# Two-layer graph kernel on one core: scatters put off around a change of batch group, first gathers spread out

## The chip, the core and the metric

The kernel runs on one core of one Trainium2 chip. The core has five engines that matter here: TensorE (matmuls, PE), VectorE (DVE), ScalarE (ACT), GpSimd (POOL) and SyncE (SP), each with its own instruction queue that is worked off in order, and 16 DMA engines that all of them share. The metric is device time in microseconds for the whole program, the median of several runs. A profiled execution gives the trace from which the profile's views come.

## The reference, cut to what matters

Two graph layers act on `x` of 16 batches x 1024 nodes x 256 features, with one adjacency matrix `adj` of 1024 x 1024 that is mostly zero.

```python
# layer 0: attention with adj as an added bias
feats = einsum('bni,oi->bno', x, W1); f1 = feats @ W2 + b2
coefs = softmax(leaky_relu(f1[:, :, None] + f1[:, None, :]) + adj)
h = coefs @ feats + bias2 + x
# layer 1: edge scores
pre_u = h @ W1[:d]; pre_v = h @ W1[d:]
S = sigmoid(relu(pre_u[:, :, None] + pre_v[:, None] + b1) @ W2 + b2)
a_t = einsum('buv,bud->bvd', S * adj, h)
m_t = einsum('uv,bud->bvd', adj, h) * h
out = beta1*h + beta2*(a_t @ Wa + ba) + beta3*(m_t @ Wm + bm)
```

The score `S` is needed only where `adj` is not zero, so the kernel works it out edge by edge.

## The kernel before, in words

**Stages.** At the start the kernel lists the edges: a table of 21 tiles, each with 128 rows (one row: a node u and up to eight nodes v). The widths of the tiles fall from 8 to 1; together they have 135 *slots*. A slot is 128 edges, one on each partition. Slot 134 is the single column of the last tile.

The 16 batches go through layer 0 one after the other. For each batch the kernel stores what the edge scores need: `pu_d` and `pw_d` (272 numbers for each node and batch: the two halves of the hidden layer, sorted by the sign of the second weight) and `ha_d` (h times Wa). Batches are scored in three groups of 5, 5 and 6 batches (groups 0, 1, 2). A group can be scored when its batches are through layer 0. So the scoring of group 0 runs beside batches 5 to 9, that of group 1 beside batches 10 to 15, and that of group 2 beside the last stage.

In the last stage TensorE does the sums over edges: it reads the scores back as dense blocks (`sat`, from the array `sa_d`, one array for each group), weighs them with `adj` (`apart`) and multiplies them with `ha_g` (matmuls `pzg` and `pzh`). The groups come there in the order 1, 0, 2. The `adj` messages of eight batches (`pm`, `pz`, stored as `zb_d`) were put off to this stage and lie between those matmuls.

**One slot.** For slot k of group g:

- `fetch(g, k)` (GpSimd): an indirect DMA gathers the rows `pw_d[v]` into a buffer `gv` (line 1219). At the first slot of a tile it also gathers `pu_d[u]` into `gu` (line 1212). There are five `gv` buffers (`GV`). Groups 0 and 1 use the same five, group 2 has five of its own in another pool (`wide`).
- `compare(k, 0)` and `compare(k, 1)` (VectorE, line 1248): maximum and minimum of `gv` and `gu`.
- `sums` (ScalarE, line 1262, one instruction for each batch; in every eighth slot of group 2 VectorE, line 1259): the sum over the 272 numbers goes to a column of `lg`.
- When a *part* of slots is complete (parts end at slots 16, 32, 48, 64, 80, 96, 112, 124, 131 and 135), `gates` (ScalarE, line 1270) and `last` (VectorE, line 1289) finish the scores, and `last` puts one scatter for each slot of the part on the list `late`. There are five `lg` buffers.
- `scatter` (GpSimd, line 1228): an indirect DMA writes 128 scores to `sa_d[g]`. The scatters of a group are declared to be independent of each other; against any other access to `sa_d[g]` the framework keeps the program's order.

**What sets the order.** The kernel's engines and queues follow the order in which instructions are emitted, and that order is written by hand. `Timetable` collects entries (time, function) and emits them sorted by time. The times are a planner's estimate; nothing waits for them on the chip. A slot's time is `start + k * (end - start) / 135`. At that time `first` fetches slot k + 3 (`AHEAD`) and issues one scatter from `late`, or two when more than 12 wait. For slot 0 `first` is due 15 us earlier: it fetches slots 0, 1, 2 and 3 at once. The loads of the last stage have times of their own, counted back from the time at which its matmuls begin (`when[0]`), and are issued by SyncE:

```python
for i, p in enumerate(parts):
    due = when[0] - 36.0 + 4.0 * i if i < SA else begins[parts[i - SA]] - 4.0
    ...
    times.at(due, lambda p=p: load_sa(*p))        # line 1332: sat <- sa_d
    times.at(begins[p] - 8.2, lambda p=p: part_sa(*p))    # ScalarE, line 1345
    times.at(begins[p] - 6.0, lambda p=p: weigh_sa(*p))   # VectorE, line 1350
```

`SA` is 7: the first seven loads have buffers of their own. Other instructions that the prediction names: `keep_product` (VectorE, line 1188, `zb`), whose store ScalarE issues (line 1194); `turn_h` (TensorE, line 1080, `ph`); `message` (TensorE, line 1158, `pm`); `keep_turned` (`xT`); `load_ha` (SyncE, line 1318, `ha_g`) and `take_up` (SyncE, line 1151, `xh`). DMAs of SyncE and ScalarE share eight lanes in turn; an issue waits until its lane's DMA before has landed. GpSimd's DMAs have eight lanes as well.

Of the kernel before, what the change touches and what calls it, by code (L numbers as in the profile page):

```python
# [29 lines left out]
SLOTS = [(t, s) for t, width in enumerate(WIDTHS) for s in range(width)]  # L30
# [341 lines left out]
def edge_layers(  # L372
# [40 lines left out]
    NG = len(GROUPS)  # L413
# [18 lines left out]
    first = first_stack.enter_context(tc.tile_pool(name="first", bufs=1, side="right"))  # L432
# [80 lines left out]
    for i in range(H):  # L513
# [5 lines left out]
        for o in range(H):  # L519
# [4 lines left out]
                start=(o == 0),  # L524
# [20 lines left out]
    many = const.tile([P, 2], F32, name="many")  # L545
# [655 lines left out]

    PARTS = [16, 32, 48, 64, 80, 96, 112, 124, 131, len(SLOTS)]
    AHEAD = GV - 2
    HA = 9
    SA = 7
    late = []

    def fetch(g, k):
        t, s = SLOTS[k]
        if s == 0:  # L1210
            gu = st["gu", t] = pools["gath", g].tile([P, SIZE[g] * R], F32, name="gu", bufs=2)
            nc.gpsimd.indirect_dma_start(
                out=gu,
                out_offset=None,
                in_=pu_d[g],
                in_offset=bass.IndirectOffsetOnAxis(ap=key_u[:, t : t + 1], axis=0),
            )
        gv = st["gv", k] = pools["gath", g].tile([P, SIZE[g] * R], F32, name="gv", bufs=GV)
        nc.gpsimd.indirect_dma_start(  # L1219
            out=gv,  # L1220
            out_offset=None,
            in_=pw_d[g],
            in_offset=bass.IndirectOffsetOnAxis(ap=idx_v[:, t, s : s + 1], axis=0),
        )

    def scatter(g, lg, i, k):
        t, s = SLOTS[k]
        dma = nc.gpsimd.indirect_dma_start(  # L1228
            out=sa_d[g],
            out_offset=bass.IndirectOffsetOnAxis(ap=idx_s[:, t, s : s + 1], axis=0),  # L1230
            in_=lg[:, i, : SIZE[g]],
            in_offset=None,
            bounds_check=N * N - 1,
            oob_is_err=False,
        )
        tc.declare_no_dep(dma.ins, group=f"sa{g}", reason="edges of their own")
        tc.add_to_no_dep_group(f"sa{g}", dma.ins)
# [4 lines left out]
    def compare(k, half):  # L1242
        if k in [0, *PARTS] and half == 0:
            st["lg"] = dense.tile([P, PARTS[0], MOST], F32, name="lg", bufs=5)
        cols, op = ((slice(0, HALF), ALU.max), (slice(HALF, R), ALU.min))[half]
        mv = by_batch(st["gv", k])[:, :, cols]
        mu = by_batch(st["gu", SLOTS[k][0]])[:, :, cols]
        nc.vector.tensor_tensor(mv, mv, mu, op)  # L1248

    def place_of(k):  # L1250

        part = next(i for i, end in enumerate(PARTS) if k < end)
        return (PARTS[part - 1] if part else 0), PARTS[part]

    def sums(k, js, lg):
        one = by_batch(st["gv", k])
        i = k - place_of(k)[0]
        if len(js) == one.shape[1]:
            nc.vector.tensor_reduce(lg[:, i, : len(js)], one, AX.X, ALU.add)
        else:  # L1260
            for j in js:
                nc.scalar.activation(  # L1262
                    one[:, j, :], one[:, j, :], AF.Copy, accum_out=lg[:, i, j : j + 1]
                )

    def gates(g, k, lg):

        k0, k1 = place_of(k)
        part = lg[:, : k1 - k0, : SIZE[g]]
        nc.scalar.activation(part, part, AF.Tanh, bias=b2_h, scale=0.5)  # L1270

    def scores(g, start, end, on_vector):

        for k in range(len(SLOTS)):
            time = start + k * (end - start) / len(SLOTS)

            def first(k=k):
                for n in range(AHEAD) if k == 0 else ():
                    fetch(g, n)
                if k + AHEAD < len(SLOTS):  # L1280
                    fetch(g, k + AHEAD)
                for _ in range(min(len(late), 2 if len(late) > PARTS[0] - 4 else 1)):
                    late.pop(0)()

            def last(k=k):
                k0, k1 = place_of(k)
                lg = st["lg", k0]
                part = lg[:, : k1 - k0, : SIZE[g]]
                nc.vector.tensor_scalar(part, part, 1.0, None, ALU.add)
                late.extend(lambda i=i: scatter(g, lg, i, k0 + i) for i in range(k1 - k0))  # L1290

            times.at(time - (15.0 if k == 0 else 0.0), first)
            times.at(time + 0.1, lambda k=k: compare(k, 0))
            times.at(time + 0.9, lambda k=k: compare(k, 1))
            k0, k1 = place_of(k)
            if k == k0:
                times.at(time + 0.2, lambda k0=k0: st.update({("lg", k0): st["lg"]}))
            summed = lambda js, k=k, k0=k0: sums(k, js, st["lg", k0])
            if on_vector(k):
                times.at(time + 1.7, lambda f=summed: f(range(SIZE[g])))  # L1300
            else:
                for j in range(SIZE[g]):
                    times.at(time + 2.0 + 0.6 * j, lambda f=summed, j=j: f((j,)))
            if k + 1 == k1:
                times.at(time + 5.4, lambda k=k, k0=k0: gates(g, k, st["lg", k0]))
                times.at(time + 6.0, last)
        ended = end + 4.0
        if g + 1 == NG:
            times.at(ended, lambda: [late.pop(0)() for _ in range(len(late))])
        return ended  # L1310
# [5 lines left out]
    def load_ha(g, c):  # L1316
        st["ha", g, c] = pools["late"].tile([P, CUT * D], F32, name="ha_g", bufs=HA)
        nc.sync.dma_start(
            out=st["ha", g, c], in_=ha_d[g][c * P : (c + 1) * P, : CUT * D]
        )  # L1320
# [133 lines left out]
    def products(b, *ids):  # L1454
        for i in ids:
            time = times.matmuls(4 * D, lambda i=i: product(b, i))
            times.at(time + 0.3, lambda i=i: keep_product(b, i))
            times.at(time + 2.3, lambda i=i: store_product(b, i))
        return time + 1.0

    times = Timetable()
# [148 lines left out]
    for n in range(3):  # L1610
# [4 lines left out]
        time = products(b, 2, 3)  # L1615
# [65 lines left out]
    for g in range(NG):  # L1681
        ended = scores(g, paced[g], paced[g + 1], lambda k, g=g: g + 1 == NG and k % 8 == 3)
# [22 lines left out]
    for n, (g, c) in enumerate((g, c) for g in order for c in range(C)):  # L1705
        if n < C:
            due = opened + 2.0 + (when[0] - 14.0 - opened) * n / C
        elif n < HA:
            due = when[2 + n - C] + 0.1
        else:  # L1710
            k, c1 = divmod(n - HA, C)
            due = begins[order[k], C - 1, c1] + 2.4
# [18 lines left out]
@with_exitstack  # L1731
def tile_graph_layers(ctx: ExitStack, tc: tile.TileContext, *args):
    nc = tc.nc
    I32 = mybir.dt.int32
    hold = ctx.enter_context(tc.tile_pool(name="hold", bufs=1))
    flag = hold.tile([1, 1], I32, name="flag")
    edge_layers(tc, *args, flag)
    over = nc.values_load(
        flag[0:1, 0:1],
        min_val=0,  # L1740
        max_val=1,
        skip_runtime_bounds_check_because="it is a comparison's result",
    )
    with tc.If(over > 0):
        dense_layers(tc, *args)
# [43 lines left out]
```

## Time and profile before

| | before |
|---|---|
| median of 3 runs (lowest to highest) | 2082.96 us (2081.66 to 2084.3) |
| profiled execution | 2087.25 us |
| its span, first to last instruction | 2085.5 us |
| PE busy | 2023.7 us, 97% |
| VectorE, ScalarE, GpSimd busy | 1569.9, 1374.0, 1137.4 us |
| granted TensorE clock, mean | 0.997 |
| gathers `gv`, GpSimd | 405, 1204 ns each |
| scatters `sa_d`, GpSimd | 405, 1257 ns each |
| comparisons, VectorE | 810, 909 ns each |
| HBM traffic over the span | 308 GB/s |

An entry such as "DVE gv L1248 <- DMA gv<-pw_d,idx_v: 106.1, 55, 12.0" in the list of waits means: VectorE's instruction of line 1248, which writes `gv`, waited for a DMA into `gv`, 106.1 us in all, in 55 places, at most 12.0 us. In a view in order of time each line has the start, the duration, engine, line, operation, output <- inputs, the number of instructions merged, and in brackets the idle time before it and what ended it. PEclk is the share of the clock that TensorE was granted. The DMA share is how busy the 16 DMA engines were. Idle time of an engine costs nothing by itself; it counts only where TensorE or the end of the program waits for it.

### The profile page before, as it was taken

What the parts mean: (1) busy time and instruction counts of PE and PEld (TensorE: products, weight loads), DVE (VectorE), ACT (ScalarE), POOL (GpSimd) and SP (SyncE); (2) the same over time, 40 slices, a digit from 0 to 9 for tenths busy, and PEclk for the clock granted to TensorE, in tenths of its full rate; (3) what the DMA queues carried; (4) which work ended last, traced back from release to release, by engine and by line L of the source; (5) the groups of instructions that cost most, each with busy time, mean ns of one, the idle gap of its engine ahead of it and who ended that gap; (6) DMA issues with size and microseconds to landing.
All of it is one profiled execution on the core that took longest, in us unless ns stands there. A gap on an engine that the chain in (4) does not pass through costs nothing.

```text
span 2085.5 us, 28967 instructions
## 1 busy us (share of the span) xinstructions
PE 2023.7 (97%) x8577; PEld 1551.1 (74%) x8577; DVE 1569.9 (75%) x2348; ACT 1374.0 (66%) x4842; POOL 1137.4 (55%) x974
## 2 busy tenths in 40 slices
PE   8999999999999999999999999899999989999998
PEld 6888887777776868677888886457676666768887
DVE  7799884677877777677878886578888878885544
ACT  4211222577777767687888777577888878886654
POOL 1122221267676767678777777666767766773000
PEclk9999999999999999999999999999999999999999
DMA  6689776788888889789999989899999999997773
GB/s 219 244 310 347 286 294 244 255 262 285 286 279 270 282 283 293 262 293 297 318 300 323 328 302 312 317 396 414 382 392 366 412 415 397 387 402 265 282 234 123
DMA packets 250007, 644.37 MB, mean 309 GB/s; under 512 B 38642, under 2 KB 139762, under 8 KB 247794
## 3 DMA queue, kind: packets, MB, share of 16 engines
q0 software_dynamic: 82016, 348.87, 47.7%
q1 hardware_dynamic: 132002, 259.36, 33.8%
q10 hardware_dynamic: 35824, 34.22, 4.7%
q8 instruction: 69, 1.13, 0.2%
q14 instruction: 96, 0.79, 0.1%
HBM read 479.56 MB, written 162.92 MB: 308 GB/s over the span
## 4 chain that ended last, share of the span: by engine, by line
PE 53%; DMA 18%; DVE 12%; ACT 8%; issue 6%; POOL 3%; SPq 0%; ACTq 0%; POOLq 0%; DVEq 0%
PE pv L1060 16%; DMA gv<-pw_d,idx_v 10%; PE pm L1158 9%; PE pp L1098 7%; PE pzg L1363 6%; DVE gv L1248 5%; PE pf L1006 4%; ACT gv L1262 4%; PE pea L1126 3%; DMA sat<-sa_d 3%; PE pzh L1363 3%; PE pz L1178 2%; ACT apart L1345 2%; DMA ha_g<-ha_d 2%; POOL sa_d L1228 2%
## 5 line engine op out<-in xcount | busy, mean ns | idle before, releaser
L1262 ACT ACTIVATE gv<-gv 128x272 f32<-128x272 f32 x2058 | 856.1, 419 | 308.2 <-DVE gv L1248 202.3
L1248 DVE TENSOR_TENSOR gv<-gv,gu 128x680 f32<-128x680 f32 (+1 forms) x810 | 706.5, 909 | 110.5 <-DMA gv<-pw_d,idx_v 106.1
L1219 POOL DMA_INDIRECT gv<-pw_d,idx_v x405 | 487.6, 1204 | 307.3 <-ACT gv L1262 197.0
L1228 POOL DMA_INDIRECT sa_d<-lg,idx_s x405 | 509.2, 1257 | 135.1 <-issue 109.5
L1060 PE MATMUL pv<-feats,eT 128*128 128x257 f32 x2048 | 468.9, 381 | 7.3 <-DVE eT L1047 6.7
L1158 PE MATMUL pm<-adj_sb,xh 128*128 128x512 f32 x1024 | 450.9, 593 | 1.7 <-DVE xh L1074 1.7
L1060 PEld LDWEIGHTS pv<-feats,eT 128*128 128x128 f32 x2048 | 381.1, 189 | 71.4 <-DVE eT L1047 14.9
L1262 ACT ACTIVATION_READ_ACCUMULATOR gv<-gv 128x1 f32 x2058 | 388.9, 189 | 0.0
L1363 PE MATMUL pzg<-ha_g,apart 128*128 128x256 f32 x1536 | 367.1, 382 | 22.2 <-DVE apart L1350 21.8
L1158 PEld LDWEIGHTS pm<-adj_sb,xh 128*128 128x128 f32 x1024 | 193.6, 191 | 220.2 <-issue 217.6
L1363 PEld LDWEIGHTS pzg<-ha_g,apart 128*128 128x128 f32 x1536 | 288.3, 190 | 83.6 <-DVE apart L1350 36.9
L1345 ACT COPY apart<-sat 128x640 f32<-128x640 f32 (+1 forms) x192 | 264.6, 1392 | 82.8 <-PE pzh L1363 38.7
L1350 DVE TENSOR_TENSOR apart<-apart,adj_sb 128x640 f32<-128x640 f32 (+1 forms) x192 | 166.3, 868 | 130.0 <-ACT apart L1345 129.4
L1098 PE MATMUL pp<-wuv,hT 128*128 128x272 f32 x1024 | 250.4, 394 | 6.7 <-ACT end L1112 3.8
L1098 PEld LDWEIGHTS pp<-wuv,hT 128*128 128x128 f32 x1024 | 194.6, 191 | 53.4 <-issue 6.2
L1047 DVE SCALAR_TENSOR_TENSOR eT<-row,col,grown 128x512 f32<-128x512 f32 x256 | 183.0, 746 | 24.6 <-ACT col L993 23.8
L852 POOL DMA_INDIRECT table_d<-rec,at x52 | 57.4, 1105 | 252.2 <-DVE rec L845 154.9
L1091 ACT COPY hT<-ph 128x512 f32<-128x512 f32 x96 | 55.2, 576 | 109.3 <-PE ph L1080 109.1
L1126 PE MATMUL pea<-wa,hT 128*128 128x256 f32 x512 | 121.4, 380 | 0.0
L1178 PE MATMUL pz<-wm,mT 128*128 128x256 f32 x512 | 116.0, 379 | 0.2 <-DVE mT L1169 0.2
L1006 PE MATMUL pf<-w1T,xT 128*128 128x257 f32 x512 | 114.1, 380 | 0.9 <-DVE xT L964 0.9
L1363 PE MATMUL pzh<-ha_g,apart 128*128 128x256 f32 x384 | 114.2, 379 | 0.0
(179 smaller groups left out, 1588.6 us busy)
## 6 DMA issues: line engine op xcount, KB each, us to landing
sa_d<-zero SPq DMA_DIRECT2D x128, 512.0 KB, 5.7
sat<-sa_d SPq DMA_DIRECT2D x128, 320.0 KB, 9.3
sat<-sa_d SPq DMA_DIRECT2D x64, 384.0 KB, 4.8
pu_d<-end SPq DMA_DIRECT2D x64, 272.0 KB, 4.9
pw_d<-end SPq DMA_DIRECT2D x64, 272.0 KB, 5.9
ha_d<-ea SPq DMA_DIRECT2D x64, 256.0 KB, 6.0
zb_d<-zb ACTq DMA_DIRECT2D x64, 256.0 KB, 6.8
xh<-in_x_dram SPq DMA_DIRECT2D x15, 1024.0 KB, 12.4
```

The lines of the kernel that those rows point to most:

```text
L1006: nc.tensor.matmul(pfs[i], lhsT=st["xT"][:, h, c * P : (c + 1) * P], rhs=w1T[:, h, :], start=(h == 0), stop=(h == H - 1),)
L1047: nc.vector.scalar_tensor_tensor(st["eT", b, k, n][:, i, :], st["row"][:, cols], st["col"][:, j : j + 1], grown[:, j, cols], ALU.max, ALU. ...
L1060: nc.tensor.matmul(pv[:, : D + 1], lhsT=st["eT", b, k, j // 4][:, j % 4, i * P : (i + 1) * P], rhs=st["feats", b][:, j, :], start=(j == 0) ...
L1098: nc.tensor.matmul(pp[:, k, :R], lhsT=st["hTi", b, i][:, h, k * P : (k + 1) * P], rhs=wuv[:, side, h, :], start=(h == 0), stop=(h == H - 1),)
L1126: nc.tensor.matmul(pp[:, k, :], lhsT=st["hTi", b, i][:, h, k * P : (k + 1) * P], rhs=wa[:, h, :], start=(h == 0), stop=(h == H - 1),)
L1158: nc.tensor.matmul(pm, lhsT=held[b][:, c, h * P : (h + 1) * P], rhs=adj_sb[:, c, span], start=(c == 0), stop=(c == C - 1),)
L1219: nc.gpsimd.indirect_dma_start(out=gv, out_offset=None, in_=pw_d[g], in_offset=bass.IndirectOffsetOnAxis(ap=idx_v[:, t, s : s + 1], axis=0),)
L1228: dma = nc.gpsimd.indirect_dma_start(out=sa_d[g], out_offset=bass.IndirectOffsetOnAxis(ap=idx_s[:, t, s : s + 1], axis=0), in_=lg[:, i, : ...
L1248: nc.vector.tensor_tensor(mv, mv, mu, op)
L1262: nc.scalar.activation(one[:, j, :], one[:, j, :], AF.Copy, accum_out=lg[:, i, j : j + 1])
L1345: nc.scalar.copy(apart.rearrange("p g v -> p v g"), sat)
L1363: nc.tensor.matmul(st["pzg", g, vc][j // 4][:, j % 4, :], lhsT=apart[:, j, :], rhs=ha, start=(c == 0 and j % 2 == 0), stop=(c == C - 1 and ...
```

## The change

Three things change in `scores`.

1. In groups 0 and 1, `first` issues no scatter in the last 14 slots (`HUSH`, slots 121 to 134).
2. In groups 1 and 2, `first` issues two scatters a slot in slots 0 to 15, as long as any are left.
3. Slots 0, 1 and 2 are fetched by entries of their own. In groups 1 and 2 they are due 15.0, 11.5 and 8.0 us before the start and the fetch of slot 3 comes with slot 0 at the start itself; in group 0 they stay together, about 15 us before it.

```diff
+    HUSH = 14
...
             def first(k=k):
-                for n in range(AHEAD) if k == 0 else ():
-                    fetch(g, n)
                 if k + AHEAD < len(SLOTS):
                     fetch(g, k + AHEAD)
-                for _ in range(min(len(late), 2 if len(late) > PARTS[0] - 4 else 1)):
+                if k + HUSH >= len(SLOTS) and g + 1 < NG:
+                    return
+                many = len(late) > PARTS[0] - 4 or (g and k < PARTS[0])
+                for _ in range(min(len(late), 2 if many else 1)):
                     late.pop(0)()
...
-            times.at(time - (15.0 if k == 0 else 0.0), first)
+            if k < AHEAD:
+                ahead = 15.0 - (3.5 * k if g else 0.01 * k)
+                times.at(start - ahead, lambda k=k: fetch(g, k))
+            times.at(time - (0.0 if g or k else 14.9), first)
```

## The prediction

> **What bounds the kernel now.** First I read the busy rows, then the waits, then TensorE, VectorE, GpSimd and SyncE in order of time around the two changes of group, then the table of stretches. TensorE works for 2023.7 us of the 2085.5 us span, so whatever the change gives must come out of TensorE's idle time. The list of waits (total us, times, longest) names the two kinds that matter:
>
> ```profile
> DVE gv L1248 <- DMA gv<-pw_d,idx_v: 106.1, 55, 12.0
> ...
> PE pzg L1363 <- DVE apart L1350: 21.8, 30, 1.8
> ...
> PE ph L1080 <- DVE zb L1188: 7.1, 2, 5.7
> ```
>
> The 7.1 us lie at the change from group 1 to group 2. TensorE there (start, us, work, wait before it):
>
> ```profile
> 1331.03 7.03 PE L1158 MATMUL pm<-adj_sb,xh 128*128 128x512 f32 x16
> 1343.79 1.11 PE L1080 MATMUL ph<-ident,xh 128*128 128x128 f32 x4 [5.73 <-DVE zb L1188]
> 1346.29 1.12 PE L1080 MATMUL ph<-ident,xh 128*128 128x128 f32 x4 [1.38 <-DVE zb L1188]
> 1347.19 8.04 PE L1158 MATMUL pm<-adj_sb,xh 128*128 128x512 f32 x16
> ```
>
> Two waits, and after them a message of 8.04 us instead of 7.03. VectorE was late because of one gather, and GpSimd's order shows which:
>
> ```profile
> 1338.58 3.48 DVE L1248 TENSOR_TENSOR gv<-gv,gu 128x680 f32<-128x680 f32 x4 [12.02 <-DMA gv<-pw_d,idx_v]
> ```
>
> ```profile
> 1318.25 0.95 POOL L1212 DMA_INDIRECT gu<-pu_d,key_u  x1 [0.30 <-issue]
> 1319.51 0.94 POOL L1219 DMA_INDIRECT gv<-pw_d,idx_v  x1 [0.30 <-issue]
> 1320.75 1.54 POOL L1219 DMA_INDIRECT gv<-pw_d,idx_v  x1 [0.30 <-issue]
> 1322.60 0.94 POOL L1219 DMA_INDIRECT gv<-pw_d,idx_v  x1 [0.30 <-issue]
> 1323.84 0.93 POOL L1219 DMA_INDIRECT gv<-pw_d,idx_v  x1 [0.31 <-issue]
> 1325.08 1.59 POOL L1228 DMA_INDIRECT sa_d<-lg,idx_s  x1 [0.30 <-DMA gv<-pw_d,idx_v]
> 1326.97 0.96 POOL L1212 DMA_INDIRECT gu<-pu_d,key_u  x1 [0.31 <-issue]
> 1328.24 0.94 POOL L1219 DMA_INDIRECT gv<-pw_d,idx_v  x1 [0.30 <-issue]
> ```
>
> Group 2's row tile and first four gathers go out in one burst, then a scatter, then the row tile and the gather (1328.24) of group 1's last slot, 134: the one VectorE needs next. It lands 10.2 us later (1338.46). The change from group 0 to 1 has the same form: the gather of slot 134 goes out at 859.70, VectorE compares at 866.7, and TensorE waits 1.68 us at 869.10 and 2.93 us at 898.08.
>
> After 1370 something else is full. The stretches (length, then PE, PEld, DVE, ACT, POOL busy, PE clock, DMA share, GB/s):
>
> ```profile
> 1340.00:1350.00 10.00, 4.83 (x13) 2.91 (x14) 9.25 (x13) 8.96 (x42) 3.87 (x3) 0.66 0.66 223
> 1390.00:1400.00 10.00, 10.00 (x33) 5.99 (x32) 7.90 (x11) 9.00 (x44) 5.49 (x5) 1.00 1.02 412
> ```
>
> From 1370 to 1880 nearly every stretch has a DMA share of 0.98 to 1.03. There the DMA engines set the pace: TensorE's 21.8 us of waits for `apart` lie there. The first of the two stretches is the stall, with a granted clock of 0.66.
>
> **The planner's clock.** Adding up the timetable's own sums (columns x 4/2400 us per matmul call) gives group starts of 387.9, 882.6 and 1351.3, slots of 3.66, 3.47 and 3.86 us, and 1437.8 for the first gather matmuls (`when[0]`). These set only the order in the queues. Real times run some 18 to 28 us earlier there: the first `pzg` runs at 1419.58.
>
> **What the change does to the queues.** No instruction is added: 405 gathers, 63 `gu` loads and 405 scatters stay. At each change of group:
>
> (a) The next group's `gu` and gather 0 still precede slot 134's, but gathers 1 and 2 come one slot apart behind it, gather 3 with slot 0. Before slot 134 the queue loses three gathers and the scatters.
>
> (b) Of the late list, 6 scatters are left at slot 121; 12+7+4 join it; so 29 wait at the new group's start (before: 13 were popped after slot 0's time). They go out two a slot, the last alone in slot 14. The five `lg` buffers are just enough: slot 16 needs the oldest, emptied by slot 3. No wait, so 0.
>
> (c) Group 1's last scatter is now due at 1351.3 + 14 x 3.86 = 1405.3. The first load of group 1's scores, `load_sa(1,0,0)`, is due at 1437.8 - 36 = 1401.8, the second at 1405.8. Before, that scatter stood at 1397.6, ahead of both. Now it comes **between** them. It writes the array that the first load reads, so I expect GpSimd to wait for that load, and the second load to wait for the scatter.
>
> **The sum, group 0 to 1.** Gone: 1.68 + 2.93 us, and the slower matmuls after (eight at about 0.22 us over their usual spacing, 1.8): -6.4. Given back: between 872.16 and 913.83 GpSimd issues 28 without pause, 1.49 us each. Three a slot and a `gu` every eighth are 4.65 us, the slot is 3.47, so it falls behind 1.2 us a slot. Starting at about 855 with 7.5 us in hand, gathers are late from slot 9 on and by some 9 us at slot 17. TensorE let VectorE's 12 us at the change of group through as 1.7 us and waited more later; I take +3.5 (0 to 6.4). Left: **-2.9** (-6.4 to 0).
>
> **Group 1 to 2, the stall.** Without the burst slot 134's gather is out some ten microseconds earlier, and the 12.02 us wait goes. TensorE: -5.73 - 1.38 - 1.5 (8.04 against 7.03, and two slow groups of transposes) = **-8.6** (-8.6 to -4, if a part of the wait for `gu` and gather 0 stays). So TensorE comes to its first `pzg` 11.5 us earlier, at about 1408.
>
> **Group 1 to 2, the hold.** What is late next is the scores. Rows of before, from GpSimd's last scatter of group 1 on (chain of waits; then issue to landing of `sat`, then of the scatters, over the whole run):
>
> ```profile
> 1381.54 8.97 DMA sa_d<-lg,idx_s
> ...
> 1390.90 8.72 DMA sat<-sa_d
> 1399.63 19.14 DMA sat<-sa_d
> ```
> ```profile
> DMA to landing us min/median/max: 3.0/7.5/20.7
> ```
> ```profile
> DMA to landing us min/median/max: 2.1/6.0/9.0
> ```
>
> In the new order: slot 0 of group 2 is compared at about 1340.1 - 12 - 2.9 = 1325; its sums free a buffer some 4 us later; twelve slots of 4.65 us bring the last scatter but one to about 1384. It lands at 1390, the first load at 1397.5, then the last scatter goes and lands at 1403.5, and only then the second load is issued, against 1390.90 before: 12.6 us later by the medians; by the least of each (7.2 us in all) 0, by the most (38.7) +32. Two queues stand still meanwhile. Behind the scatter on GpSimd wait the gathers from slot 18 on: out at 1399 instead of 1392.0, landed about 1407, where VectorE came to them at 1402.3. Behind the second load on SyncE wait all `sat`, `ha_g` and `xh` loads, and through the eight shared DMA lanes a store of `zb` on ScalarE that went out at 1418.85. The first `sat` of the second half landed at 1418.77, 27.9 us after the second load's issue; the same spacing gives 1431.4, and with the copy (1.3) and the weighing (0.8) TensorE starts that half at about 1433.5 instead of 1431.66. So TensorE's lead of 11.5 us is used up: **+13.5** (0 to +25). As the DMA engines are full before and after, what stays is the 5 to 6 us in which the hold leaves them little to do, less some 3 us that earlier gathers and `ha_g` loads had brought: +2.5, the same size.
>
> Sum: -2.9 - 8.6 + 13.5 = **+2.0 us** on the profiled execution's 2087.25 us (2085.5 span and 1.75 around it). That execution is 4.3 us (0.2%) above the median of the runs, 2082.96; carried to the median: **2085 us**.
>
> **A rule against the change.** The rows show gathers standing behind whatever GpSimd waits for. The Trainium skill, "DMA: Bandwidth & Descriptors", section "Anatomy of one DMA — SWDGE (gpsimd) path", says why: the DMA engines do not wait on semaphores, the issuing sequencer does, before dispatch. The same section puts one DMA at about 2.0 us plus its bytes over 436 GB/s; as an estimate from that page the first load (328 KB) would take 2.8 us and a scatter 2.0, the hold would be 6.8 us and the sum some -10; the trace's 8.72 and 8.97 us under load speak against using it.
>
> **Rivals.** *Faster, 0.29:* the hold is near the least landings, or that scatter does not wait for the load at all; the second load goes out at about 1391 as before and TensorE keeps part of its 11.5 us. For it: least landings sum to 7.2 us, and GpSimd's queue is drained by then. Against: the full DMA stage hands a lead of TensorE back, so of -11.5 I leave -5 to -11: about 2075. *Slower, 0.33:* the hold is under load, 9.0 + 14.3 (median `sat` landing between 1300 and 1480) + 9.0 = 32 us; the second load goes at 1416, 25 us late, gathers 20 us late. One place, one price: the queues held at the first load; it decides when the hold passes about 20 us. TensorE waits over 3 us there again and its clock falls as at 1340; +5 to +13: about 2091. *The change does not do what it says, inside the forecast:* three issues a slot make GpSimd the bound in group 1 and the stall only moves to slots 9 to 18: -6.4 becomes 0.
>
> **How the numbers follow.** Forecast, no change within 0.2% (4.2 us, about what a measurement of this kernel can tell): 0.38, its own range 2079 to 2087. Faster 0.29, slower 0.33. The range 2074 to 2096 takes in most of both rivals.
>
> **What would show it.** Right: no TensorE wait over 3 us where group 1 ends; VectorE's longest wait for a gather well under 12 us there; a GpSimd scatter waiting for `sat<-sa_d` for over 8 us at about 1385 to 1400; the second `sat` issue past 1397; waits of `pzg` for `apart` near 1410 to 1435. Wrong: the scatter goes out without a wait, two `sat` issues side by side as now, and the first `pzg` at 1408 followed by no waits (faster); or waits of 10 us and more for `apart`, or a long wait in slots 9 to 18 of group 1 (slower).

## The result, and the profile after

| | before | after |
|---|---|---|
| median (lowest to highest), 6 runs each | 2083.63 us (2079.47 to 2090.87) | 2100.35 us (2099.27 to 2104.63) |
| profiled execution | 2087.25 us | 2104.63 us |
| its span | 2085.5 us | 2102.9 us |
| mean granted clock | 0.997 | 0.993 |

The ratio is 1.0075 (95% interval 1.0061 to 1.0089): some 16 us slower, outside the range of 2074 to 2096 us. Ratios here and below are the recorded ones, of executions in the chip's fast state alone, so they can differ a little from the quotient of the medians beside them (e2: 2130.39/2119.91 is 1.0049, recorded is 1.0027).

The list of waits of the changed kernel (total us, times, longest), answering to the first fence of the prediction:

```profile
DVE gv L1249 <- DMA gv<-pw_d,idx_v: 115.7, 53, 8.1
...
PE pzg L1368 <- DVE apart L1355: 22.3, 29, 2.7
...
PE pzg L1368 <- issue: 9.8, 1, 9.8
```

The wait of `ph` for `zb` is gone, and VectorE's longest wait for a gather is 8.1 us, no longer 12.0. A new line has come: TensorE stands 9.8 us before a `pzg`. TensorE in order of time, first where group 1 ends, then at the first scores:

```profile
1333.67 1.04 PE L1080 MATMUL ph<-ident,xh 128*128 128x128 f32 x8
1334.55 7.03 PE L1158 MATMUL pm<-adj_sb,xh 128*128 128x512 f32 x16
...
1434.04 3.75 PE L1368 MATMUL pzg<-ha_g,apart 128*128 128x256 f32 x8 [9.76 <-issue]
```

Eight transposes in one go, no bracket, a message of 7.03 us: the stall that the change is aimed at is gone. At 1434.04 TensorE has waited 9.76 us, and its first eight `pzg` take 3.75 us where the next eight take 1.89 us (granted clock 0.74 from 1420 to 1440).

The profile names no releaser for the 9.76 us ("issue"), but VectorE's order shows what came last:

```profile
1421.70 1.94 DVE L1249 TENSOR_TENSOR gv<-gv,gu 128x816 f32<-128x816 f32 x2 [8.07 <-DMA gv<-pw_d,idx_v]
...
1433.12 0.81 DVE L1355 TENSOR_TENSOR apart<-apart,adj_sb 128x640 f32<-128x640 f32 x1
```

The weighing of the first scores ends at 1433.93, 0.1 us before TensorE starts. VectorE had stood 8.07 us for a gather before it.

GpSimd, then SyncE, at the hold that the prediction named (a wait put down to `mT`, which had long been written; by its semaphore it is the landing of the first `sat` at 1413.22):

```profile
1413.98 0.99 POOL L1229 DMA_INDIRECT sa_d<-lg,idx_s  x1 [8.79 <-DVE mT L1169]
```
```profile
1407.83 8.58 SPq L1337 DMA_DIRECT2D sat<-sa_d  x2
```

The two `sat` issues are 8.26 us apart (1407.83 and 1416.09; before 1390.53 and 1390.90), with group 1's last scatter at 1413.98 between them. The gathers that VectorE needed next stood behind that scatter and went out from 1415.27 on: the hold reached the first `pzg` by way of the gathers and VectorE, while the first load had landed some 20 us before. So far the order of the queues is as predicted. The second load goes out at 1416.09, where the slower rival had it (1416), but by luck: in e15, where group 1 is not late, it goes out at 1402.22.

What the prediction did not have is the time at which TensorE comes there. The next table is worked out from the order of time: the start of a batch's first attention matmul (`pv`), of the first `pzg`, of the second half of the scores and of the last half, each less its time in the profile of before (us). Each row is one execution; that of e13 took 5.5 us more than its median and that of e15 3.4 us less, so a few microseconds in a single entry mean little. The rows below the changed kernel's are the experiments of the two sets in which the kernel before took about as long (2086.49 and 2084.79 us); their medians and ratios stand with each experiment.

| run | batch 10 | 11 | 12 | 15 | first `pzg` | 2nd half | last half |
|---|---|---|---|---|---|---|---|
| time before | 835.7 | 937.6 | 1026.6 | 1217.7 | 1419.6 | 1431.7 | 2068.0 |
| changed kernel | +0.9 | +9.8 | +11.7 | +14.3 | +14.4 | +20.0 | +17.4 |
| the same again (e5) | +0.3 | +9.0 | +10.0 | +12.3 | +10.7 | +15.7 | +14.9 |
| three scatters in two slots (e6) | 0.0 | +1.4 | +7.4 | +8.2 | +9.6 | +15.0 | +13.7 |
| burst kept at group 1 (e7) | +0.1 | +10.9 | +11.1 | +12.8 | +11.8 | +16.9 | +14.7 |
| 14 scatters left out (e13) | 0.0 | -0.3 | 0.0 | -0.2 | -0.7 | +4.8 | +6.4 |
| 7 slots without scatters (e16) | -0.1 | +5.6 | +5.8 | +6.5 | +7.0 | +12.5 | +9.7 |
| gathers apart only, both (e14) | +0.7 | +2.0 | +1.9 | +0.5 | -7.1 | -7.1 | -8.7 |
| gathers apart only, group 2 (e8) | +1.0 | +2.2 | +2.1 | +2.8 | -5.5 | -4.5 | -5.5 |
| change at group 2 only (e15) | +0.9 | +1.2 | +1.3 | +0.9 | +0.4 | +5.8 | +1.0 |

In the changed kernel 9 to 14 us are lost between batch 10 and batch 15, beside the start of group 1, where the prediction expected a gain of 2.9 us. TensorE's waits there are many and short, with matmuls at a lower clock between them (0.95 from 855 to 950, before 0.98):

```profile
898.55 3.50 PE L1098 MATMUL pp<-wuv,hT 128*128 128x272 f32 x8 [3.76 <-ACT xT L962]
...
929.52 0.69 PE L974 MATMUL pr<-ident,f 128*128 128x128 f32 x2 [3.40 <-DVE f L1023]
```

None of them names a gather, but VectorE does. GpSimd's gather of slot 16, before and after, then VectorE's comparison of that slot after the change:

```profile
910.47 1.65 POOL L1219 DMA_INDIRECT gv<-pw_d,idx_v  x1 [0.30 <-issue]
```
```profile
921.69 1.30 POOL L1220 DMA_INDIRECT gv<-pw_d,idx_v  x1 [0.30 <-DMA sa_d<-lg,idx_s]
```
```profile
928.46 0.93 DVE L1249 TENSOR_TENSOR gv<-gv,gu 128x680 f32<-128x680 f32 x1 [5.33 <-DMA gv<-pw_d,idx_v]
```

VectorE stands 5.33 us for this gather; `f` stands behind it in its queue and runs at 929.32, and `pr`, which needs `f`, at 929.52. The gather is *issued* 11.2 us late. From the issue to the comparison it is 6.8 us, before 6.9: the transfer took no longer.

### The profile page after: what moved, and what is told of

It is laid out like the page before. It is cut to its first block, busy times and chain, and to the rows that moved or that the text cites. A ratio compares the mean times of both kernels' runs of the same rounds, so it can differ in the third digit from the quotient of the medians.

```text
span 2102.9 us, 28967 instructions
## 1 busy us (share of the span) xinstructions
PE 2029.6 (97%) x8577; PEld 1555.0 (74%) x8577; DVE 1568.0 (75%) x2348; ACT 1375.4 (65%) x4842; POOL 1130.5 (54%) x974
## 4 chain that ended last, share of the span: by engine, by line
PE 55%; DVE 13%; DMA 12%; ACT 10%; issue 6%; POOL 2%; SPq 0%; ACTq 0%; POOLq 0%; DVEq 0%
PE pv L1060 18%; PE pm L1158 10%; PE pp L1098 8%; DVE gv L1249 5%; PE pzg L1368 5%; ACT gv L1263 5%; DMA gv<-pw_d,idx_v 5%; PE pea L1126 4%; PE pf L1006 3%; ACT apart L1350 3%; DMA sat<-sa_d 3%; PE pz L1178 3%; PE pzh L1368 2%; DVE eT L1047 1%; DVE apart L1355 1%
## 5 line engine op out<-in xcount | busy, mean ns | idle before, releaser
L1220 POOL DMA_INDIRECT gv<-pw_d,idx_v x405 | 478.5, 1182 | 297.0 <-ACT gv L1263 181.3
L1060 PEld LDWEIGHTS pv<-feats,eT 128*128 128x128 f32 x2048 | 382.0, 190 | 69.3 <-DVE eT L1047 11.7
L1213 POOL DMA_INDIRECT gu<-pu_d,key_u x63 | 77.5, 1230 | 93.1 <-PE pv L1060 41.9
```

The lines of the kernel that those rows point to most:

```text
L1060: nc.tensor.matmul(pv[:, : D + 1], lhsT=st["eT", b, k, j // 4][:, j % 4, i * P : (i + 1) * P], rhs=st["feats", b][:, j, :], start=(j == 0) ...
L1220: nc.gpsimd.indirect_dma_start(out=gv, out_offset=None, in_=pw_d[g], in_offset=bass.IndirectOffsetOnAxis(ap=idx_v[:, t, s : s + 1], axis=0),)
```

## The experiments: the change from group 0 to group 1

The diffs are against the changed kernel. Three theories stand against each other: **Q**, the GpSimd time of the scatters that are put off; **W**, the wait of 9.30 us at the row tile of slot 134, with three gathers behind it; **the spacing** of the gathers itself. The wait for W, on GpSimd of the changed kernel:

```profile
855.84 1.21 POOL L1213 DMA_INDIRECT gu<-pu_d,key_u  x1 [9.30 <-DVE gv L1249]
```

**e5: the changed kernel again**, as a yardstick on one chip with e6, e7 and e8.

> The changed kernel, not edited, as the yardstick for the three beside it: its ratio to the kernel before was 1.0075 (+16 us). Every theory expects the same again, 1.006 to 1.009, with TensorE 10 to 13 us late at the attention of batch 12 and 14 to 21 us late from the second half of the scores on. If the ratio comes out under 1.005, the chip adds something of its own to both and only the differences among these four runs are to be read.

Measured: 2103.67 us beside 2086.49, ratio 1.0096 (1.0079 to 1.0113), just above the range expected.

**e7: the burst kept at the start of group 1.**

```diff
-                ahead = 15.0 - (3.5 * k if g else 0.01 * k)
+                ahead = 15.0 - (3.5 * k if g in (2,) else 0.01 * k)
...
-            times.at(time - (0.0 if g or k else 14.9), first)
+            times.at(time - (0.0 if g in (2,) or k else 14.9), first)
```

> The change, but at the start of group 1 the first four gathers go out in one burst ahead of slot 134's row tile as in the kernel before; scatters and group 2 as in the change. Theory Q (GpSimd's issue time): three gathers of 1.25 us use time in which GpSimd otherwise stands at the row tile, so 3.75 us of the backlog go; TensorE at batch 12 is 7 to 9 us late instead of 11.7, the whole 2 to 5 us faster than the changed kernel. Rival W (the wait at the row tile with the gathers behind it is the whole loss): the gathers are ahead of the wait again, the lateness at batch 12 goes nearly whole (0 to 3 us), the whole is 8 to 12 us faster than the changed kernel. Rival B (the burst delays slot 134's gather): 1.7 and 2.9 us of stalls come back, 1 to 5 us slower than the changed kernel.

Measured: 2101.77 us, ratio 1.0084 (1.0068 to 1.0101), 1.9 us below e5; batch 12 is 11.1 us late. W falls: three gathers ahead of the row tile change next to nothing. So does B: the kernel is not slower than e5. Q's size fails too, and GpSimd's order of time shows why:

```profile
858.07 0.97 POOL L1220 DMA_INDIRECT gv<-pw_d,idx_v  x1 [0.30 <-issue]
869.06 0.94 POOL L1220 DMA_INDIRECT gv<-pw_d,idx_v  x1 [10.03 <-ACT gv L1263]
```

With the three gathers issued early, the next one waits 10.03 us for one of the five `gv` buffers. GpSimd can't use this time for gathers; only scatters could fill it, and these stand behind the gather.

**e6: three scatters in two slots in group 1**, two in even slots and one in odd ones.

```diff
                 many = len(late) > PARTS[0] - 4 or (g and k < PARTS[0])
+                many = many and (g != 1 or k % 2 == 0)
```

> The change with the scatters left over from group 0 going out three in two slots (two in even slots, one in odd ones) all through group 1; group 2 as in the change. Theory Q (GpSimd's queue has no time for three issues a slot: 4.65 us of issuing against slots of 3.47 us; 16 slots put the gathers some 11 us late, and a lateness that lasts many slots reaches TensorE whole): now 2.5 issues and an eighth of a row tile cost about 3.8 us a slot, GpSimd keeps up within 0.3 us a slot, TensorE is at most 5 us late at batch 12 (changed kernel: 11.7 us), and the whole is 6 to 12 us faster than the changed kernel, 2088 to 2094 us beside a kernel before of 2083 (ratio 1.002 to 1.005). Rival W (what is lost is the 9.3 us that GpSimd stands at the row tile of slot 134, with the next gathers behind it): that wait is unchanged, TensorE is 8 us late or more at batch 12, and the whole is within 4 us of the changed kernel.

Measured: 2101.47 us, ratio 1.0087 (1.0068 to 1.0105), 2.2 us below e5. Batch 11 is on time (+1.4 us), batch 12 is 7.4 us late and batch 15 8.2. So the rate of three issues a slot sets *when* the loss comes, not whether it comes. My price for the rate alone was wrong: spreading the scatters gave back 2 us instead of 6 to 12. By the numbers set beforehand W came nearer here; e7 and e13 decide against it.

**e13: 14 of the scatters left out**, the second one of each of group 1's first 14 slots (so the scores of 14 slots of group 0 are missing from the result).

```diff
-                for _ in range(min(len(late), 2 if many else 1)):
-                    late.pop(0)()
+                for n in range(min(len(late), 2 if many else 1)):
+                    do = late.pop(0)
+                    if not (g == 1 and k < 14 and n):
+                        do()
```

> The changed kernel, in which the second scatter of each of group 1's first 14 slots is left out (14 of group 0's last rows of scores are never written, so that part of the result is missing); order and waits of all the rest are the change's. Theory Q (what costs in group 1 is the GpSimd time of the scatters that were put off, about 1.4 us each, 20 us in all): TensorE is at most 4 us late at batch 12 and at most 5 us at batch 15, where the changed kernel is 10 to 12 and 12 to 14 us late, and the whole is 8 to 12 us faster than the changed kernel, ratio to before 1.003 to 1.005. Rival W (the wait at slot 134's row tile with three gathers behind it, which stays): TensorE is 8 us late or more at batch 12 and the whole within 4 us of the changed kernel.

Measured: 2088.51 us beside 2084.79, ratio 1.0009 (0.9991 to 1.0027). Batch 12 is 0.0 us late and batch 15 -0.2, with the row tile's wait in place (8.59 us). Q holds for group 1: nothing else of the change costs anything visible there. The whole is faster than Q had expected (1.003 to 1.005), and faster than the change at group 2 alone (e15, 1.0038); why was not found out. The stretches 700 to 855 and 855 to 950 (length, then PE, PEld, DVE, ACT, POOL busy, clock, DMA share, GB/s), before, changed, e13:

```profile
700.00:855.00 155.00, 155.00 (x648) 117.02 (x647) 115.90 (x189) 116.84 (x491) 110.49 (x95) 1.00 0.88 293
855.00:950.00 95.00, 90.40 (x362) 65.88 (x361) 68.71 (x111) 68.74 (x291) 66.53 (x57) 0.98 0.82 269
```
```profile
700.00:855.00 155.00, 155.00 (x648) 117.02 (x647) 117.73 (x192) 117.78 (x492) 95.52 (x81) 1.00 0.87 292
855.00:950.00 95.00, 84.21 (x336) 62.26 (x335) 62.43 (x101) 63.20 (x263) 71.90 (x63) 0.95 0.76 239
```
```profile
700.00:855.00 155.00, 155.00 (x648) 117.02 (x647) 119.07 (x193) 117.92 (x496) 96.48 (x82) 1.00 0.87 290
855.00:950.00 95.00, 91.47 (x363) 66.93 (x362) 65.87 (x106) 68.80 (x291) 68.22 (x56) 0.96 0.85 276
```

Read the POOL column: the hush takes 15 us of work out of group 0's end, where TensorE was at 155.00 of 155 us anyway, and moves it behind 855. With the 0.30 us that GpSimd leaves after each issue it has 95 - 66.53 - 57 x 0.30 = 11.4 us to spare there before, 4.2 us in the changed kernel and 10.0 in e13; from 700 to 855 it has 16.0 us before and 35.2 after. The DMA share is lower there in the changed kernel (0.76 against 0.82), so the DMA engines were not what was short. Leaving a scatter out removes its traffic as well as GpSimd's time; that it is GpSimd's time rests on this share and on slot 16's rows above, where the gather is late at its issue and not in its transfer.

**e16 and e10: 7 slots without scatters in group 0** instead of 14.

```diff
-                if k + HUSH >= len(SLOTS) and g + 1 < NG:
+                if k + (HUSH if g else 7) >= len(SLOTS) and g + 1 < NG:
```

> The change, but only the last 7 slots of group 0 go without scatters instead of 14; group 1's start and group 2 as in the change. Theory Q (a dose): half of the scatters stay in GpSimd's idle time, so half of the loss goes: TensorE 4 to 7 us late at batch 12 instead of 10 to 12, the whole 4 to 7 us faster than the changed kernel (2096 to 2099 where that took 2103). Rival W: the row tile's wait is the same, no more than 2 us faster.

> The change with only the last 7 slots of group 0 without scatters, again, as the first run's interval was 10 us wide. Theory Q as a dose (half of the scatters put off, half of the loss): TensorE 4 to 8 us late at batches 12 to 15, whole 4 to 7 us faster than the changed kernel, ratio 1.0045 to 1.0065. Theory S (GpSimd's spare time, some 12 us of the first 95 of group 1, takes seven scatters, 10 us, whole): under 3 us late at batch 15, ratio 1.001 to 1.004. Rival W: as the changed kernel within 2 us.

Measured: e10 2120.86 beside 2107.44 us, 1.0065 (1.0042 to 1.0088); e16 2098.33 beside 2084.79 us, 1.0065 (1.0045 to 1.0086). In e16 batch 15 is 6.5 us late, against 12.3 and 14.3 with 14 slots and 0.5 to 2.8 with none: about 0.9 us for each scatter put off. The dose holds by the profile, and S (seven scatters fit into the spare time) falls. Of the 11.4 us to spare before, about half lies ahead of 880, in GpSimd's waits for a buffer (1.06 us at 859.70, 5.06 us at 870.88); from 880 to 900 nothing is left (15.73 us busy and 15 gaps of 0.30 us in 20 us). The medians are too wide to show the 4 to 7 us against the changed kernel: the intervals overlap. Against the change at group 2 alone in the same set the seven scatters cost 6.4 us (e16, e15) and 5.3 us (e10, e11) by medians. The profile of e10 does not show the dose: it loses 23.1 us from batch 10 to 15, others of its set 19.6 to 24.9 without a hush in group 0 (see the last section).

**e14 and e9: only the first gathers apart**, in groups 1 and 2, no scatter put off.

```diff
-                if k + HUSH >= len(SLOTS) and g + 1 < NG:
-                    return
-                many = len(late) > PARTS[0] - 4 or (g and k < PARTS[0])
+                many = len(late) > PARTS[0] - 4
```

> The kernel before with the first gathers of both later groups a slot apart, and nothing else: no scatter is put off, two a slot only as before. Theory Q (what costs at the change from group 0 to 1 are the scatters that are put off: GpSimd stands idle 35 us of 700 to 855 instead of 16 us, and the 13 scatters, 19 us, come on top of a group in which it has no more than some 30 us of spare time): nothing is lost there, TensorE at most 4 us later than before at batch 12, and the whole is like the run with the first gathers of group 2 apart alone (4.8 us faster than before), within 3 us. Rival W (the gathers behind the wait for slot 134's row tile): TensorE is 6 us late or more at batch 12 and the whole 2 us or more slower than before.

> The first gathers of both later groups a slot apart and no scatter put off, once more, since the interval of the first run (0.997 to 1.0022) leaves its sign open. Theory Q: like the run with group 2's first gathers apart alone (0.9977), or up to 4 us faster than that where the two short stalls at the start of group 1 go as well: ratio 0.996 to 0.998, TensorE within 3 us of before at batch 12 and 6 to 9 us nearer to it at the second half of the scores than at batch 15. Rival W (gathers apart cost at the start of group 1): 1 us or more behind apart alone, ratio 0.999 or above, TensorE 6 us late or more at batch 12.

Measured: e9 2106.37 beside 2107.44 us, 0.9996 (0.997 to 1.0022), its sign open; e14 2078.68 beside 2084.79 us, 0.9977 (0.996 to 0.9993). In e14 batch 12 is 1.9 us late and batch 15 0.5: the spacing costs nothing at group 1, and it gains nothing there (waits of 2.29 us at 870.41 and 1.92 us at 900.06 remain, where before had 1.68 and 2.93).

**e2: the change at the start of group 1 alone** (group 2 as before), run with e1, e3 and e4.

```diff
-                if k + HUSH >= len(SLOTS) and g + 1 < NG:
+                if k + HUSH >= len(SLOTS) and g + 1 in (1,):
...
-                many = len(late) > PARTS[0] - 4 or (g and k < PARTS[0])
+                many = len(late) > PARTS[0] - 4 or (g in (1,) and k < PARTS[0])
...
-                ahead = 15.0 - (3.5 * k if g else 0.01 * k)
+                ahead = 15.0 - (3.5 * k if g in (1,) else 0.01 * k)
...
-            times.at(time - (0.0 if g or k else 14.9), first)
+            times.at(time - (0.0 if g in (1,) or k else 14.9), first)
```

> The change only where group 0 gives way to group 1; group 1 to 2 as before. Theory M (three issues a slot and gathers 1 to 3 behind the wait for the row tile put group 1 behind its pace): batch 11 starts some 9 us late, batch 15 some 14, the stall at the change from group 1 to 2 stays, and the time is 2092-2098. Rival D (the full DMA stage swallows what is lost or won before 1400): 2083-2087. The prediction's own term for this part was -2.9: 2080.

Measured: 2130.39 us beside 2119.91 on that chip, 1.0027 (1.0 to 1.0055). From batch 10 to 15 TensorE loses 42.2 us in this run, where the two of the same set without the hush in group 0 (e3, e4) lose 26.9 and 19.6. The sign fits Q, and the interval leaves out the -2.9 us of the prediction (a ratio of 0.9986); the size can't be read in this set (see the last section).

## The experiments: the change from group 1 to group 2

**e8: only group 2's first gathers apart.** The diff is that of e14, with `g in (2,)` in place of `g` in the two lines of the spacing.

> The kernel before with one part of the change: group 2's first gathers stand a slot apart; no scatter is put off, two a slot only as before, group 1's start as before. So the 5.7 and 1.4 us stalls at the end of group 1 should go (VectorE no longer waits 12 us for the gather of slot 134) while the scores' last scatters stay where they were. Theory L (TensorE's lead is kept when no load of scores is put off): 6 to 10 us faster than the kernel before, ratio 0.995 to 0.997. Theory D (the DMA engines are full from 1370 to 1880 and set the end: what TensorE gains before it stands still for later): within 3 us of the kernel before, TensorE some 8 us early at the first pzg and level at the start of the last group's scores near 1910. If the scatters of slots 121 to 134, which stand between the gathers as before, delay slot 134's gather themselves, the stall stays above 2 us.

Measured: 2080.54 us beside 2086.49, ratio 0.9977 (0.9968 to 0.9986): the fastest kernel here beside e14, and 5.9 us faster than before. TensorE goes from 2.8 us late at batch 15 to 5.5 us early at the first `pzg`, and is 5.5 us early at the end. L holds, and D falls: a lead at 1430 is not handed back between 1430 and 1900, though the DMA share is 0.99 to 1.02 from 1430 to 1800 (0.87 from 1800 to 1900). e14 says the same (7.1 us early at 1431.7, 8.7 at the end).

**e15, e11 and e3: the change at group 2 alone**, three times. The diff is that of e2 with `(2,)` for `(1,)`.

> The change only where group 1 gives way to group 2, the last scatter still between the first two loads. H and M: the 5.7 us and 1.4 us stalls near 1343 go, the hold costs 12-15 us instead: 2084-2090, batches 11 to 15 as before. If instead the hold is the whole loss: 2096-2100. If it costs nothing: 2074-2078.

> The change at the change of group 1 to 2 alone (group 0's scatters and group 1's start as before), once more, since the chip of the first such run was 1.7% slower for every kernel and its intervals were wide. Theory Q: no loss in group 1, so some 10 to 14 us faster than the changed kernel, and beside the run with the first gathers apart alone (4.8 us faster than before) it shows the price of the scatters that are put off in group 1, the hold among it. Theory H (the hold: GpSimd and the score loads stand 8 to 15 us): 6 to 10 us slower than those apart alone, that is 1 to 5 us slower than before, with 8 us of wait at the first pzg. Rival N (the hold costs nothing, as the DMA engines are full afterwards): within 2 us of apart alone, ratio 0.997 to 0.999.

> The change at the change of group 1 to 2 alone, a third time, for the size of the two parts beside each other on one chip (1.0014 and 1.004 before, both with wide intervals). Theory Q: TensorE not late at batch 15 by more than 4 us, then 3 to 5 us lost between batch 15 and the end (the stall gone, the hold and the later scatters in its place): whole 2 to 7 us slower than before, ratio 1.001 to 1.0035. If the whole loss of the change lay at group 2, it would be 12 us or more.

Measured: e3 2125.5 beside 2119.91 us, 1.0014 (0.9985 to 1.0043); e11 2115.59 beside 2107.44 us, 1.004 (1.002 to 1.0059); e15 2091.89 beside 2084.79 us, 1.0038 (1.0024 to 1.0052). In e15's set the scatters put off in group 1 cost 2091.89 - 2078.68 = 13.2 us against e14 (which also spreads group 1's first gathers, about nothing by batch 15). The rows of e15: GpSimd, SyncE, TensorE:

```profile
1390.04 1.00 POOL L1229 DMA_INDIRECT sa_d<-lg,idx_s  x1 [0.30 <-issue]
1400.10 1.00 POOL L1229 DMA_INDIRECT sa_d<-lg,idx_s  x1 [7.78 <-DVE gv L1249]
```
```profile
1395.86 6.68 SPq L1337 DMA_DIRECT2D sat<-sa_d  x2
```
```profile
1420.00 3.75 PE L1368 MATMUL pzg<-ha_g,apart 128*128 128x256 f32 x8 [8.83 <-issue]
```

SyncE of e14 at the same place:

```profile
1384.83 0.80 SPq L1335 DMA_DIRECT2D sat<-sa_d  x2
```

In e14 both loads go out within 0.80 us from 1384.83, and TensorE comes to its first `pzg` at 1412.46 without a wait. In e15 the first goes out 11.0 us later, because group 1's scatters end later, and the second 6.4 us after the first (1402.22), because of the hold. So there are two delays, 11.0 and 6.4 us.

**e12, e4 and e1: three scatters in slot 13 of group 2**, so that the last scatter of group 1 stands ahead of the first load and no scatter waits for a load. e12 and e4 have the change at group 2 alone, e1 the whole change.

```diff
-                for _ in range(min(len(late), 2 if many else 1)):
+                for _ in range(min(len(late), 2 + (g == 2 and k == 13) if many else 1)):
```

> The changed kernel, but slot 13 of group 2 issues three scatters, so that group 1's last scatter stands ahead of the first load of its scores instead of between the first two. Theory H (the hold: GpSimd waits for the first load, SyncE for the scatter): the 8.8 us wait of GpSimd and the 8.3 us between the first two loads go, TensorE's 9.8 us wait near 1424 goes or shrinks under 3 us, and the time falls from 2100 to 2086-2091. Rival D (the full DMA engines of the last stage decide, the hold only shows where): the wait turns up later in the stage, 2096-2100.

> As the one before, with three scatters in slot 13, so that the last one stands ahead of the first load. H and M: neither loss is left and the stall near 1343 is gone: 2074-2079, faster than both kernels. Rival D (a lead of TensorE is handed back in the full DMA stage): 2081-2085.

> The same with three scatters in slot 13, so that group 1's last scatter stands ahead of the first load of its scores and no scatter waits for that load. Theory H: the hold is gone and with it most of its price, 3 to 8 us faster than the run beside it and within 3 us of apart alone. Rival P (what costs is that group 1's last scatters come two slots later and under a queue of three issues a slot, whether one of them stands between the loads or not): within 2 us of the run beside it, the first load of the scores still 8 us or more later than before, and TensorE still waits over 5 us at its first scores.

Measured: e1 2132.92 beside 2119.91 us, 1.0047 (1.0024 to 1.007), where 2086 to 2091 us beside 2083.63 had been expected, at most 1.0035; e4 2126.9 beside 2119.91 us, 1.0016 (0.9995 to 1.0037), 1.4 us above e3; e12 2110.21 beside 2107.44 us, 1.0014 (0.9991 to 1.0037), 5.4 us below e11. By medians the price of the hold stays open: the two pairs disagree and their intervals overlap. SyncE and TensorE of e12:

```profile
1417.40 0.85 SPq L1337 DMA_DIRECT2D sat<-sa_d  x2
```
```profile
1443.58 3.78 PE L1368 MATMUL pzg<-ha_g,apart 128*128 128x256 f32 x8 [4.58 <-DVE apart L1355]
```

The hold is gone (two issues in 0.85 us), but TensorE still waits for its first scores: 2.63 us at the first `pzg` (1436.61) and 4.58 us at the second eight. The profiles give this: from batch 15 to the end, against before, TensorE loses 0.1 to 6.6 us in the ten runs with the hold (mean 3.3), changes by -3.2 to +1.9 in the three with slot 13 (mean -1.0), and gains 8.3 to 9.5 us in e8, e9 and e14 (mean 9.0). By these means the hold costs 3.3 + 1.0 = 4.3 us and the later scatters 9.0 - 1.0 = 8.0. But they mix sets. Within one set the profiles put 5.3 us (e11 against e12) and 1.3 us (e3 against e4) on the hold and 7.8 us on the later scatters (e12 against e9), while the medians of e11, e12 and e9 put 5.4 us on the hold and 3.8 on the scatters. Both cost something; how the price divides, and so whether H or P is nearer, stays open.

## Why the prediction was wrong

**Group 0 to 1: -2.9 us predicted, 9 to 14 us lost. This is the step that failed.** It failed in one sentence: "Starting at about 855 with 7.5 us in hand, gathers are late from slot 9 on and by some 9 us at slot 17. TensorE let VectorE's 12 us at the change of group through as 1.7 us and waited more later; I take +3.5 (0 to 6.4)." The lateness of the gathers was right: VectorE compares slot 17 at 931.6 instead of 922.4, 9.2 us late, slot 16 11.1 us late and slot 24 13.0. What was wrong is how much of it reaches TensorE. The "12 us" here were two waits of 8.25 and 3.75 us, of which TensorE waited 1.68 us and later 2.93; at the other change of group 12.02 us became 7.1. So single late gathers reached TensorE in part; a lateness that every slot has from slot 9 on reaches it whole: TensorE at batch 12 is 11.7 us late. The upper end of 6.4 us was only the size of the gain beside it; no row gave it.

The term on the other side, -6.4 us, was not there either. The stall was put down to three gathers and the scatters ahead of slot 134. But slot 134's row tile waits for a buffer until slot 133 has been compared, so without them its gather goes out at 857.35 instead of 859.70, 2.35 us earlier, and VectorE's wait for it shrinks only from 8.25 to 7.32 us. With the hush's work left out (e13) or never put off (e14), batch 11 is at -0.3 and +2.0 us, not at -6.4.

The rival that named this, "three issues a slot make GpSimd the bound in group 1 and the stall only moves", had the place and the engine right and the size wrong: it let the gain become 0. It is also not the rate alone (e6): what is lost is GpSimd's idle time before the change of group, 15 us of busy time moved from a stretch in which nothing waited for it into one without room.

**Group 1 to 2, the stall: -8.6 us predicted, right.** From batch 15 to the first `pzg` e14 gains 7.6 us and e8 8.3 (1.36 and 0.70 us of the waits for `zb` remain). In the changed kernel both waits are gone as well; the 9.76 us wait at the first `pzg` takes their place, so batch 15 and the first `pzg` show the same lateness (14.3 and 14.4).

**Group 1 to 2, the hold: +13.5 us predicted, 13.2 us measured (e15 against e14); the hold is there, the size is luck.** Predicted was the second load at 1403.5; in e15, where group 1 is not late, it goes out at 1402.22. But I expected the last scatter but one at 1384 and 13.5 us from its landing to the second load. It came at 1390.04, and from there on the hold took 6.4 us (8.3 in the changed kernel). Two errors of 6 to 7 us cancelled; the prediction had the first load on time (1390, before 1390.53) and the whole delay in the hold, while in e15 the load itself is at 1395.86. The estimate from the Trainium skill, "DMA: Bandwidth & Descriptors", section "Anatomy of one DMA — SWDGE (gpsimd) path", was 2.8 + 2.0 us for the two parts of this wait; the section gives its fit for DMAs that GpSimd issues, and the load is issued by SyncE. The rows of the changed kernel are 5.39 us for the load (1407.83 to 1413.22) and 2.10 for the scatter (1413.98 to 1416.08), between the page's estimate and the 7.5 and 6.0 of the median landings that I used. The DMA engines were running empty by then (share 0.94 from 1400 to 1410, 0.35 from 1410 to 1420), so medians over the whole run were the wrong rows.

**What TensorE's lead is worth.** The prediction let the full DMA stage hand a lead back ("so of -11.5 I leave -5 to -11") and took +2.5 for the lateness that remains by the DMA engines. Both runs with a lead (e8, e14) keep it whole. The lateness after the hold mostly stays: +20.0 us at the second half, +17.4 at the end; only in e15 most of it goes (+5.8, then +1.0).

**The sum.** With measured terms: 12 to 14 for group 1's start (e5 and the changed kernel, batch 10 to 15), 3.3 from there to the end (the mean above, the stall's gain in it): 15 to 17 us, against the 16 that the medians show. This adds up the same profiles and is no independent test.

## What to carry to other kernels

Work taken off a queue just ahead of a critical place must be done later. Count the idle time of that engine on both sides, and where in the stretch it lies: here 15 us of scatters left a stretch where GpSimd's time was free and came into one with 11 us to spare in 95, about half of it in waits for a buffer. Here a delay of many slots in a row went through to the bounding engine whole, where a single late transfer of about the same size went through in part. A stall that has one cause (a burst of gathers ahead of one that is needed) is best mended at that cause alone: the gathers apart, without the rest of the change, gave 0.9977 twice (e8, e14; a third run, e9, leaves the sign open).

## What the runs showed of the hardware

The sets of runs differ, each taken on another chip; whether the chip is the cause is not shown. The kernel before took 2083.63, 2086.49 and 2084.79 us beside the changed kernel, e5 to e8 and e13 to e16, and 2119.91 and 2107.44 us in the sets of e1 to e4 and e9 to e12. In the profiles of these two sets VectorE and ScalarE stand still for up to 13 us with a releaser that no profile of the others has. In the list of waits of e2:

```profile
DVE mT L1169 <- remote: 13.2, 1, 13.2
```

Such lines add up to 78 us on the two engines in e2. TensorE loses 20 to 27 us from batch 10 to 15 there even without a hush in group 0 (e3, e4, e9, e11, e12), so sizes from these sets hold only between runs of one set, and for batches 10 to 15 hardly there. What the releaser is was not found out.
